# Output projection of a switch-head attention layer: turned and projected two chunks at a time, one turn per expert

## The chip, the cores and the metric

The kernel runs on one core of a Trainium2 chip. The metric is device time in microseconds (us): from a launch to its end, taken as the median of several executions. One further execution was recorded by the hardware profiler; all instruction times below come from that one and are counted from the start of its span.

## The reference, cut to what matters

Two sequences (B = 2) of T = 2048 positions with D = 256 features. The first layer is a recurrent network over blocks of 128 positions; its result is `x1`. The second layer, where the change lies, is attention with H = 8 heads of width DH = 64 whose values and outputs go through E = 5 experts:

```python
v = einsum('bthe,btek->bhtk', wv, xv)           # values: mix of the experts chosen per head
probs = softmax(q @ k.T)                        # per head, over all 2048 positions
attn = einsum('bhij,bhjd->bihd', probs, v)
out = einsum('bthe,bthk,ekd->btd', mask_o, attn, Wo)
x = x1 + out
```

The last einsum is what the change rewrites. For each position, `y[e, k]` is the sum over heads of `mask_o[h, e] * attn[h, k]`: 5 x 64 = 320 numbers. The output row is these 320 numbers times `Wo`, seen as a 320 x 256 matrix, plus `x1`.

## The kernel before, in words

**Tiles and stages.** A chunk is 128 positions; a sequence has NCH = 16 of them. A unit is one head and one block of 512 queries (4 chunks), so there are 64 units: 32 for each sequence, the 8 heads in order, 4 blocks in each head. The attention runs as a software pipeline of NT = 256 turns, 4 turns for each unit, written out by hand (`tc.manual_schedule()`), so the order of instructions on each engine is the order of the program. In every turn:

- TensorE makes two score tiles (`scores`, L642). Their matmuls contract 64 rows and make 32 columns: two halves of the array's rows and four groups of its columns, eight tiles of the array in all.
- ScalarE copies the scores out of PSUM (`stage`, L654) and VectorE keeps a running maximum (`largest`, L664).
- GpSimd or VectorE subtracts the maximum (`subtract`, L710) and ScalarE takes the exponential (`exponential`, L713), both for tiles made LAG = 6 turns earlier.
- TensorE multiplies by the values (`products`, L723; tiles of 128 rows by 32 columns, four of them), and every second turn adds up the softmax's denominator (`sums`, L744, same tile shape, into the one PSUM buffer "d").
- GpSimd issues a DMA that adds one exponentiated tile onto its neighbour (`fold`, L735), so `sums` needs half as many matmuls; `sums` waits for that DMA.

**End of a unit.** `take` and `take_sums` move the products and the denominator from PSUM to SBUF tile `os`. `close` (through `weigh`) transposes `os`, divides, and multiplies by the output masks (`masked`, L789), giving `pro`, 128 positions x 4 chunks x 5 experts x 64. For the first seven heads `gather` adds `pro` to a DRAM buffer `yd` by DMA; for the eighth, `fetch_y` loads the sum so far into `y`, and `gather` adds `pro` to it on GpSimd (L846).

**The output of a chunk.** `turn_out` transposes `y` of one chunk, 320 columns, in pieces of 128, 128 and 64 (three TensorE transposes, L859, into PSUM tile `py`), and ScalarE copies the pieces to `yT` (L863 for the two full ones, L866 for the half one). `yT` is one of two fixed buffers in SBUF pool "big". `turn_out` also issues the load of `z`, the chunk of `x1`, on SyncE's queue, unless it was loaded ahead (`load_z`, tile `zz`, four chunks at once). `project_out` then runs 3 x 4 matmuls of 128 rows by 32 columns on `wo` (L885) into `pz`, VectorE adds `z` (L893), and SyncE's queue stores the result (L894).

**Where this stands in the order.** Four tables (`before`, `between`, `first_behind`, `behind`) hold extra calls for a turn. Calls in `before` come ahead of the turn's products, calls in `behind` after them. The outputs of the first sequence are made between turns 126 and 142. Those of the second begin in turns 254 and 255 and end in `drain()`, a hand-written list after the last turn, which also finishes the last three units (called w, v and u there). The PSUM pool "m" (`misc`) has two buffers shared by all small tiles. In `drain()` the scores' PSUM is free, and a pool of four more buffers (`other`, tag "z") takes its place; the flag `spare` tells the two cases apart. `close_last` finishes the last unit and interleaves it with the last chunks' outputs.

**Queues.** SyncE's queue is in order: loads and stores wait in it for what they need, and everything behind waits too. GpSimd's fold DMAs stand in line with its subtractions in the same way.

Of the kernel before, what the change touches and what calls it, by code (L numbers as in the profile page):

```python
# [14 lines left out]
P = 128  # L15
# [5 lines left out]
def pass_over(  # L21
# [50 lines left out]
    yd = dram.tile([B, T // 512, P, 4, E, DH], F32, name="yd" + mark)  # L72
# [27 lines left out]
    wo = const.tile([P, (ED + P - 1) // P, D], F32, name="wo")  # L100
# [6 lines left out]
    wo_rows = Wo.rearrange("e k d -> (e k) d")  # L107
    o_chunks = [(i, min(P, ED - i)) for i in range(0, ED, P)]
    nc.vector.memset(wo[:, len(o_chunks) - 1, :], 0.0)
    for i, (r0, n) in enumerate(o_chunks):  # L110
        nc.sync.dma_start(out=wo[0:n, i, :], in_=wo_rows[r0 : r0 + n, :])
# [454 lines left out]
    big = ctx.enter_context(tile_pool(name="big", bufs=1))  # L566
# [23 lines left out]
    def experts(b, c):  # L590

        pv = misc([P, E, DH], f"pv{b}_{c}")
        by_quarters(pv.rearrange("p e k -> p (e k)"), b, c, wv.rearrange("p c e k -> p c (e k)"))
        xw = ap.tile([P, DH, E], F32, tag="xw", bufs=2, name=f"xw{b}_{c}")
        nc.scalar.copy(xw, pv.rearrange("p e k -> p k e"))
        nc.sync.dma_start(out=xvd[b, c // 4, :, c % 4], in_=xw)
# [191 lines left out]
    def masked(dst, po, mr, s, n):  # L788
        nc.vector.tensor_tensor(  # L789
            dst,  # L790
            po[:, s : s + n, 0:DH].unsqueeze(2).to_broadcast([P, n, E, DH]),
            mr[:, s : s + n].unsqueeze(3).to_broadcast([P, n, E, DH]),
            ALU.mult,
        )

    def close(u):

        i, n = units[u]
        b, h = heads[i]
        po, mr = weigh(u)  # L800
        pr = four.tile([P, QS, E, DH], F32, tag="pro", bufs=1, name=f"pro{u}")
        masked(pr, po, mr, 0, QS)
        o_of["p", u] = pr

    def fetch_y(u):

        i, n = units[u]
        b, _ = heads[i]
        y_of[b, n] = four.tile([P, QS, E, DH], F32, tag="y", bufs=2, name=f"y{b}_{n}")
        nc.sync.dma_start(out=y_of[b, n], in_=yd[b, n])  # L810

    def close_last(u, outs):

        i, n = units[u]
        b, _ = heads[i]
        po, mr = weigh(u)
        y = y_of[b, n]
        pr = four.tile([P, QS, E, DH], F32, tag="pro", bufs=1, name=f"pro{u}")
# [29 lines left out]
    yT_of = {"n": 0}  # L848
# [5 lines left out]
    def turn_out(b, c):  # L854
        yf = y_of[b, c // QS][:, c % QS].rearrange("p e k -> p (e k)")
        py = other(f"py{b}_{c}")[:, : len(o_chunks) * P] if spare else misc([P, len(o_chunks) * P], f"py{b}_{c}")
        py = py.rearrange("p (k n) -> p k n", n=P)
        for k, (r0, m) in enumerate(o_chunks):
            nc.tensor.transpose(py[0:m, k, :], yf[:, r0 : r0 + m], ident)  # L859
        yT = yT_all[yT_of["n"] % 2]  # L860
        yT_of["n"] += 1
        full = sum(m == P for _, m in o_chunks)
        nc.scalar.copy(yT[:, 0:full, :], py[:, 0:full, :])  # L863
        for k, (r0, m) in enumerate(o_chunks):
            if m < P:
                nc.scalar.copy(yT[0:m, k, :], py[0:m, k, :])  # L866
        z = yT_of.pop(("z", b, c), None)
        if z is None:
            z = ap.tile([P, D], F32, tag="z", bufs=3, name=f"z{b}_{c}")
            nc.sync.dma_start(out=z, in_=x1d[c, :, b, :])  # L870
        yT_of[b, c] = (yT, z)
# [8 lines left out]
    def project_out(b, c, at_end=False):  # L880
        yT, z = yT_of.pop((b, c))
        pz = other(f"pz{b}_{c}")[:, :D] if at_end else misc([P, D], f"pz{b}_{c}")
        for k, (r0, m) in enumerate(o_chunks):
            for g in range(0, P, 32):
                nc.tensor.matmul(  # L885
                    pz[g : g + 32],
                    lhsT=yT[:, k, g : g + 32],
                    rhs=wo[:, k, :],
                    start=k == 0,
                    stop=k == len(o_chunks) - 1,  # L890
                    tile_position=(0, g),
                )
        nc.vector.tensor_tensor(z, pz, z, ALU.add)  # L893
        nc.sync.dma_start(out=out[b].rearrange("(n s) d -> s n d", s=NCH)[c], in_=z)  # L894
# [4 lines left out]
    def load_late(b, c):  # L899
        late["x", c] = ap.tile([P, D], F32, tag="xl", name=f"xl{b}_{c}_{len(late)}")  # L900
        nc.sync.dma_start(out=late["x", c], in_=x1d[c, :, b, :])
# [91 lines left out]
    for b in range(1, B):  # L993

        T0 = (b - 1) * H * H_T + 2 * LAG + 3
        for c in range(NCH):
            T = T0 + c // 2 * U_T
            at(behind, T - 2 + c % 2, load_late, b, c)
            at(between, T + c % 2, stats_late, b, c)
        T0 += NCH // 2 * U_T  # L1000
        for part in range(2):
            at(behind, T0 + 3, scales_late, b, part)
            T0 += U_T
        for c in range(NCH):
# [12 lines left out]
        assert T0 <= b * H * H_T  # L1017
    for u, (i, n) in enumerate(units):
# [4 lines left out]
        outs = [(b, n * QS + s) for s in range(QS)]  # L1023
# [6 lines left out]
        if h == H - 1 and n < NQ - 3:  # L1030
            T = T1 + LAG + 4
            for o, t, p in zip(outs, (0, 1, 3, 3), (1, 2, 3, 4)):
                if T + t < NT:
                    at(before if o[1] % QS == 2 else behind, T + t, turn_out, *o)
                if T + p < NT:
                    at(behind if o[1] % QS == 2 else before, T + p, project_out, *o)
        if h == H - 1 and b < B - 1 and n >= NQ - 3:
            T = T1 + LAG + 4
            for o, t, p in zip(outs, (0, 1, 3, 3), (1, 2, 3, 4)):
                at(before if o[1] % QS == 2 else behind, T + t, turn_out, *o)  # L1040
                at(behind if o[1] % QS == 2 else before, T + p, project_out, *o)

    def drain():
# [4 lines left out]
        outs = [(B - 1, c) for c in range(NCH)]  # L1048
        turned, projected = 2, 1

        def turn(n=1):
            nonlocal turned
            for _ in range(n):
                turn_out(*outs[turned])
                turned += 1

        def project(n=1):
            nonlocal projected
            for _ in range(n):
                project_out(*outs[projected])  # L1060
                projected += 1

        load_z(B - 1, NQ - 3)
        load_z(B - 1, NQ - 2)
        spread_max(v)
        turn_max(u)
# [16 lines left out]
        turn()  # L1083
# [8 lines left out]
        turn()  # L1092
        fetch_y(v)
        project()
        load_z(B - 1, NQ - 1)
# [13 lines left out]
        turn()  # L1109
# [9 lines left out]
        project()  # L1119
# [20 lines left out]
        turn()  # L1140
        project()
        turn()
        close_last(u, outs[-QS - 2 :])
# [117 lines left out]
```

## Time and profile before

| | us |
|---|---|
| median of 3 runs | 1560.38 (1559.92 to 1560.54) |
| profiled execution, its own time | 1562.38 |
| its span | 1560.5 |
| TensorE busy | 1513.2 |
| VectorE busy | 1300.0 |
| GpSimd busy | 1287.0 |
| ScalarE busy | 1245.4 |
| 384 matmuls of the output projection, mean of one record | 0.379 |

A matmul in float32 is recorded as two instructions, so the 384 matmuls of L885 stand as 768. Matmuls overlap: what one costs is not its recorded duration but the distance between the starts of the groups. "Idle before, releaser" in a row names what ended the wait of an engine. The granted TensorE clock (PEclk) is given as a share of full speed.

### The profile page before, as it was taken

The page shows a single profiled execution, that of the slowest core. Times are in us where ns is not written, and L with a number is a line of the kernel's source. Part 1 is how long each engine was busy: PE and PEld are TensorE (multiplying, and loading weights), DVE is VectorE, ACT ScalarE, POOL GpSimd, SP SyncE. Part 2 cuts the span into 40 slices and gives each one's busy share as a digit, 9 for nine tenths or more (in the row PEclk, how much of TensorE's full clock was granted, in tenths as well). Part 3 has the DMA queues.
Part 4 walks back from the last instruction along what each step waited for, and adds up shares of the span by engine and source line. Part 5 has one row for each costly group of instructions (what it writes and reads, how often), then busy time and mean ns, then how long its engine had stood idle before and what let it go on. Part 6 is the DMA issues. An engine that isn't in the chain of part 4 may idle for free.

```text
span 1560.5 us, 41474 instructions
## 1 busy us (share of the span) xinstructions
PE 1513.2 (97%) x17582; PEld 534.4 (34%) x17582; DVE 1300.0 (83%) x1811; ACT 1245.4 (80%) x1617; POOL 1287.0 (82%) x855
## 2 busy tenths in 40 slices
PE   6999899999999999999999999999999999999988
PEld 5984222222233333333223332222222222222233
DVE  7474899999988877888987779999999999899873
ACT  4674688888888888888887778888888888888863
POOL 3154699999999987999997778899999999999970
PEclk9999999999999999999999999999999999999999
DMA  5021478888888887788786777888888888888963
GB/s 167 1 109 40 114 163 196 190 189 176 177 178 179 183 183 162 163 178 179 160 200 156 167 161 176 175 178 176 175 177 179 175 179 180 174 170 176 195 163 92
DMA packets 86821, 254.15 MB, mean 163 GB/s; under 512 B 11808, under 2 KB 31072, under 8 KB 86624
## 3 DMA queue, kind: packets, MB, share of 16 engines
q0 software_dynamic: 43488, 164.65, 57.9%
q1 hardware_dynamic: 41504, 86.13, 16.6%
q8 instruction: 140, 2.29, 0.6%
q10 hardware_dynamic: 1632, 0.61, 0.2%
q14 instruction: 57, 0.47, 0.1%
HBM read 59.46 MB, written 50.33 MB: 70 GB/s over the span
## 4 chain that ended last, share of the span: by engine, by line
PE 63%; DVE 19%; ACT 7%; issue 5%; DMA 3%; POOL 1%; ACTq 0%; SPq 0%; DVEq 0%; POOLq 0%
PE s L642 21%; PE o L723 17%; DVE m L664 11%; ACT p L654 5%; PE d L744 4%; DVE pro L789 3%; PE pq L166 3%; PE pk L147 3%; PE pz L885 2%; PE phb L368 2%; PE px L309 1%; PE pha L368 1%; DMA p<-p 1%; DMA z<-x1d 1%; ACT p L713 1%
## 5 line engine op out<-in xcount | busy, mean ns | idle before, releaser
L710 POOL TENSOR_TENSOR p<-p,top 128x1024 f32<-128x1024 f32 x378 | 1005.1, 2759 | 25.8 <-ACT top L703 25.5
L654 ACT COPY p<-s 128x1024 f32<-128x1024 f32 x512 | 511.5, 1012 | 139.6 <-issue 60.8
L713 ACT ACTIVATE p<-p 128x1024 f32<-128x1024 f32 x512 | 538.8, 1064 | 51.3 <-DVE p L710 42.7
L642 PE MATMUL s<-q,k 64*32 64x512 f32 x4096 | 501.6, 596 | 4.9 <-ACT p L654 2.5
L642 PE MATMUL s<-qs,k 64*32 64x512 f32 x4096 | 501.6, 596 | 3.5 <-ACT p L654 1.8
L723 PE MATMUL o<-p,v 128*32 128x512 f32 x4096 | 492.4, 598 | 5.1 <-DVE os L760 4.3
L664 DVE TENSOR_TENSOR m<-s,m 128x1024 f32<-128x1024 f32 x320 | 390.7, 1221 | 85.5 <-PE s L642 76.1
L735 POOL DMA_DIRECT2D p<-p x254 | 259.9, 1023 | 103.2 <-issue 43.7
L723 PEld LDWEIGHTS o<-p,v 128*32 128x32 f32 x4096 | 114.0, 109 | 301.5 <-issue 158.9
L642 PEld LDWEIGHTS s<-q,k 64*32 64x32 f32 x4096 | 100.5, 106 | 156.0 <-ACT p L654 60.3
L642 PEld LDWEIGHTS s<-qs,k 64*32 64x32 f32 x4096 | 100.4, 106 | 154.2 <-ACT p L654 58.1
L710 DVE TENSOR_TENSOR p<-p,pt 128x1024 f32<-128x1024 f32 x126 | 152.4, 1210 | 0.0
L744 PE MATMUL d<-p,ones 128*32 128x512 f32 x1032 | 136.3, 592 | 1.6 <-DMA p<-p 1.6
L664 DVE TENSOR_TENSOR m<-s,p 128x1024 f32<-128x1024 f32 x64 | 78.4, 1225 | 50.5 <-ACT p L654 49.6
L789 DVE TENSOR_TENSOR pro<-po,mr 128x1280 f32<-128x1280 f32 (+1 forms) x67 | 95.9, 1431 | 3.2 <-DVE mr L785 0.5
L626 DVE TENSOR_TENSOR xq<-xq,wp 128x1280 f32<-128x1280 f32 x60 | 89.2, 1487 | 2.1
L632 DVE TENSOR_REDUCE v<-xq 128x256 f32<-128x1280 f32 x60 | 88.5, 1475 | 0.0
L166 PE MATMUL pq<-xn2T,wq 128*32 128x512 f32 x512 | 62.2, 598 | 0.0
L147 PE MATMUL pk<-xn2T,wk 128*32 128x512 f32 x512 | 61.5, 598 | 0.0
L744 PEld LDWEIGHTS d<-p,ones 128*32 128x32 f32 x1032 | 34.0, 110 | 79.9 <-issue 76.0
L843 POOL DMA_DIRECT2D yd<-pro x48 | 60.1, 1252 | 0.0
L403 POOL TENSOR_TENSOR x<-x,hvb 128x512 f32<-128x512 f32 x14 | 17.8, 1275 | 45.8 <-ACT hs L376 34.2
(178 smaller groups left out, 1492.3 us busy)
## 6 DMA issues: line engine op xcount, KB each, us to landing
p<-p POOLq DMA_DIRECT2D x254, 512.0 KB, 5.4
xq<-xvd SPq DMA_DIRECT2D x60, 640.0 KB, 4.3
yd<-pro POOLq DMA_DIRECT2D x48, 640.0 KB, 6.5
qs<-q SPq DMA_DIRECT2D x64, 128.0 KB, 4.8
yd<-pro SPq DMA_DIRECT2D x8, 640.0 KB, 5.9
y<-yd SPq DMA_DIRECT2D x8, 640.0 KB, 8.2
x<-in_x SPq DMA_DIRECT2D x16, 256.0 KB, 5.8
x1d<-x SPq DMA_DIRECT2D x16, 256.0 KB, 2.0
```

The lines of the kernel that those rows point to most:

```text
L147: nc.tensor.matmul(pk[at_col : at_col + 32], lhsT=wk[:, kc, h * DH + g : h * DH + g + 32], rhs=xc[:, kc, c0 // 2 : (c0 + HC) // 2, o, :], ...
L166: nc.tensor.matmul(pq[at_col : at_col + 32, :], lhsT=wq[:, kc, h * DH + g : h * DH + g + 32], rhs=xn2T[:, kc, b, n * QB : (n + 1) * QB], s ...
L626: nc.vector.tensor_tensor(xq, xq, wp.unsqueeze(2).to_broadcast([P, 4, DH, E]), ALU.mult)
L642: nc.tensor.matmul(ss[g : g + 32, o, :], lhsT=k_of[i][half, c, g : g + 32], rhs=q_of[i, n][o][half, :], start=True, stop=True, tile_positi ...
L654: nc.scalar.copy(p, ss)
L664: nc.vector.tensor_tensor(m, ss, ring[t - 1] if c == 1 else m, ALU.max)
L710: eng.tensor_tensor(p, p, top.unsqueeze(1).to_broadcast([P, 2, QB]), ALU.subtract)
L713: nc.scalar.activation(ring[t], ring[t], AF.Exp)
L723: nc.tensor.matmul(o_of[u][at_col : at_col + 32, :], lhsT=v_of[i][:, 2 * c + o, g : g + 32], rhs=ring[t][:, o, :], start=c == 0, stop=c == ...
L735: nc.gpsimd.dma_start(out=ring[t], in_=ring.pop(t + 1), accum_op=ALU.add)
L744: nc.tensor.matmul(den_of[u][32 * g : 32 * (g + 1), :], lhsT=ones32, rhs=ring[(t, t1)[g // 2]][:, g % 2, :], start=first, stop=last, tile_ ...
L789: nc.vector.tensor_tensor(dst, po[:, s : s + n, 0:DH].unsqueeze(2).to_broadcast([P, n, E, DH]), mr[:, s : s + n].unsqueeze(3).to_broadcast ...
```

## The change

Outputs are made for pairs of chunks. Four things change together.

- **Layout.** `pro`, `y` and `yd` are ordered expert, chunk, 64 instead of chunk, expert, 64. So for one expert two neighbouring chunks lie side by side: 128 columns.
- **One turn per expert.** `turn_out` does one transpose of 128 columns per expert, five for a pair: the first chunk's 64 land on partitions 0 to 63, the second chunk's on 64 to 127. They are made in two parts (experts 0 to 2, experts 3 and 4), with one ScalarE copy each.
- **Projection on row halves.** `wo` holds every expert's 64 rows twice, on partitions 0 to 63 and on 64 to 127. `project_out` makes both chunks at once: for each expert, one chunk's four matmuls on the upper half of the array's rows and the other's on the lower half, into two PSUM buffers: 40 matmuls of 64 rows by 32 columns for a pair instead of 24 of 128 by 32.
- **Buffers and order.** `yT` takes space of other tags ("sg" in the turns, ring "p0" in the drain), `xw`, `z` and the late input tiles share one tag "w" of four buffers, the pool "big" is gone. The extra calls stand in a table `PLACES`; in the turns one of the two projections puts its second chunk in the denominators' buffer "d". In `drain()` the calls are reordered: `x1` of chunks 2 and 3 is loaded at its start (`load_z1`), the other loads of `x1` come later, and the addition `y + pro` of unit v runs on VectorE instead of GpSimd. `close_last` makes its two pairs ready two chunks at a time.

```diff
-    yd = dram.tile([B, T // 512, P, 4, E, DH], F32, name="yd" + mark)
+    yd = dram.tile([B, T // 512, P, E, 4, DH], F32, name="yd" + mark)
...
-    wo = const.tile([P, (ED + P - 1) // P, D], F32, name="wo")
+    wo = const.tile([P, E, D], F32, name="wo")
...
-    nc.vector.memset(wo[:, len(o_chunks) - 1, :], 0.0)
-    for i, (r0, n) in enumerate(o_chunks):
-        nc.sync.dma_start(out=wo[0:n, i, :], in_=wo_rows[r0 : r0 + n, :])
+    for p0 in range(0, P, DH):
+        nc.sync.dma_start(out=wo[p0 : p0 + DH], in_=Wo.rearrange("e k d -> k e d"))
...
-        xw = ap.tile([P, DH, E], F32, tag="xw", bufs=2, name=f"xw{b}_{c}")
+        xw = ap.tile([P, DH, E], F32, tag="w", bufs=4, name=f"xw{b}_{c}")
...
     def masked(dst, po, mr, s, n):
         nc.vector.tensor_tensor(
             dst,
-            po[:, s : s + n, 0:DH].unsqueeze(2).to_broadcast([P, n, E, DH]),
-            mr[:, s : s + n].unsqueeze(3).to_broadcast([P, n, E, DH]),
+            po[:, s : s + n, 0:DH].unsqueeze(1).to_broadcast([P, E, n, DH]),
+            mr[:, s : s + n].rearrange("p s e -> p e s").unsqueeze(3).to_broadcast([P, E, n, DH]),
             ALU.mult,
         )
...
         def ready(s):
-            masked(pr[:, s : s + 1], po, mr, s, 1)
-            nc.vector.tensor_tensor(y[:, s], y[:, s], pr[:, s], ALU.add)
+            masked(pr[:, :, s : s + 2], po, mr, s, 2)
+            nc.vector.tensor_tensor(y[:, :, s : s + 2], y[:, :, s : s + 2], pr[:, :, s : s + 2], ALU.add)
         ready(0)
-        project_out(*outs[0])
-        ready(1)
+        project_out(*outs[0], True)
+        turn_out(*outs[1])
+        ready(2)
         project_out(*outs[1], True)
-        for s in range(QS):
-            turn_out(*outs[2 + s])
-            if s + 2 < QS:
-                ready(s + 2)
-            if s:
-                project_out(*outs[1 + s], s % 2 == 0)
-        project_out(*outs[-1], True)
+        turn_out(*outs[2])
+        project_out(*outs[2], True)
...
-            nc.gpsimd.tensor_tensor(y, y, pr, ALU.add)
-    yT_all = [big.tile([P, len(o_chunks), P], F32, name=f"yT{k}") for k in range(2)]
-    for yT in yT_all:
-        nc.gpsimd.memset(yT[:, len(o_chunks) - 1, :], 0.0)
...
+            eng = nc.vector if spare and n == NQ - 2 else nc.gpsimd
+            eng.tensor_tensor(y, y, pr, ALU.add)
+    PARTS = ((0, E // 2 + 1), (E // 2 + 1, E))
+    def turn_out(b, c, parts=(0, 1)):
+        y = y_of[b, c // QS]
+        if 0 in parts:
+            if spare:
+                yT = ap.tile([P, 2, QB], F32, tag="p0", bufs=RING[0], name=f"yT{b}_{c}")
+                yT = yT.rearrange("p o q -> p (o q)")[:, : E * P].rearrange("p (e n) -> p e n", n=P)
+            else:
+                yT = ap.tile([P, E, P], F32, tag="sg", bufs=2, name=f"yT{b}_{c}")
+            yT_of[b, c] = yT
+            for o in range(2):
+                if ("z", b, c + o) not in yT_of:
+                    load_z1(b, c + o)
+        yT = yT_of[b, c]
+        for e0, e1 in [PARTS[part] for part in parts]:
+            nm = f"py{b}_{c}_{e0}"
+            py = (other(nm) if spare else misc([P, QB], nm))[:, : (e1 - e0) * P]
+            py = py.rearrange("p (e n) -> p e n", n=P)
+            for e in range(e0, e1):
+                nc.tensor.transpose(
+                    py[:, e - e0, :],
+                    y[:, e, c % QS : c % QS + 2, :].rearrange("p s k -> p (s k)"),
+                    ident,
+                )
+            nc.scalar.copy(yT[:, e0:e1, :], py)
+    def load_z1(b, c):
+        yT_of["z", b, c] = ap.tile([P, D], F32, tag="w", bufs=4, name=f"z{b}_{c}")
+        nc.sync.dma_start(out=yT_of["z", b, c], in_=x1d[c, :, b, :])
...
+    def project_out(b, c, at_end=False, sums_bank=False):
+        yT = yT_of.pop((b, c))
+        pzs = []
...
+        for e in range(E):
+            for o, pz in enumerate(pzs):
+                half = slice(o * DH, (o + 1) * DH)
+                for g in range(0, P, 32):
+                    nc.tensor.matmul(
+                        pz[g : g + 32],
+                        lhsT=yT[half, e, g : g + 32],
+                        rhs=wo[half, e, :],
+                        start=e == 0,
+                        stop=e == E - 1,
+                        tile_position=(o * DH, g),
+                    )
+        for o, pz in enumerate(pzs):
+            z = yT_of.pop(("z", b, c + o))
+            nc.vector.tensor_tensor(z, pz, z, ALU.add)
+            nc.sync.dma_start(out=out[b].rearrange("(n s) d -> s n d", s=NCH)[c + o], in_=z)
...
+    PLACES = [
+        (behind, 0, turn_out, 0, (0,)),
+        (before, 1, turn_out, 0, (1,)),
+        (before, 2, project_out, 0, False, True),
+        (behind, 3, turn_out, 2, (0,)),
+        (before, 4, turn_out, 2, (1,)),
+        (behind, 5, project_out, 2),
+    ]
...
     def drain():
...
+        for c in range(2, QS):
+            load_z1(B - 1, c)
         load_z(B - 1, NQ - 3)
-        load_z(B - 1, NQ - 2)
         spread_max(v)
+        turn()
         turn_max(u)
...
         gather(w)
-        turn()
         exponential(tu)
...
         fold(tv + 6)
-        turn()
         fetch_y(v)
-        project()
-        load_z(B - 1, NQ - 1)
+        load_z(B - 1, NQ - 2)
         take(v)
...
         exponential(tu + 4)
-        turn()
         project()
...
         turn()
-        project()
         exponential(tu + 6)
         products(tu + 4)
         products(tu + 5)
         exponential(tu + 7)
-        turn()
         fetch_y(u)
-        project()
+        load_z(B - 1, NQ - 1)
         close(v)
         gather(v)
+        project()
         products(tu + 6)
         products(tu + 7)
         take(u)
-        project()
...
         turn()
         turn()
         project()
-        turn()
-        project()
-        turn()
-        close_last(u, outs[-QS - 2 :])
+        close_last(u, outs[-3:])
```

More of the change, by code (lines that the diff above doesn't have):

```diff
@@ L106, in pass_over @@
         )
-    wo_rows = Wo.rearrange("e k d -> (e k) d")
-    o_chunks = [(i, min(P, ED - i)) for i in range(0, ED, P)]
-    nc.vector.memset(wo[:, len(o_chunks) - 1, :], 0.0)
-    for i, (r0, n) in enumerate(o_chunks):
-        nc.sync.dma_start(out=wo[0:n, i, :], in_=wo_rows[r0 : r0 + n, :])
+    for p0 in range(0, P, DH):
+        nc.sync.dma_start(out=wo[p0 : p0 + DH], in_=Wo.rearrange("e k d -> k e d"))
     ones32 = const.tile([P, 32], F32, name="ones32")
@@ L565, in pass_over @@
     RING = (LAG + 4, LAG + 3)
-    big = ctx.enter_context(tile_pool(name="big", bufs=1))
     ap = ctx.enter_context(tile_pool(name="attn", bufs=2))
@@ L800, in close @@
         po, mr = weigh(u)
-        pr = four.tile([P, QS, E, DH], F32, tag="pro", bufs=1, name=f"pro{u}")
+        pr = four.tile([P, E, QS, DH], F32, tag="pro", bufs=1, name=f"pro{u}")
         masked(pr, po, mr, 0, QS)
@@ L808, in fetch_y @@
         b, _ = heads[i]
-        y_of[b, n] = four.tile([P, QS, E, DH], F32, tag="y", bufs=2, name=f"y{b}_{n}")
+        y_of[b, n] = four.tile([P, E, QS, DH], F32, tag="y", bufs=2, name=f"y{b}_{n}")
         nc.sync.dma_start(out=y_of[b, n], in_=yd[b, n])
@@ L817, in close_last @@
         y = y_of[b, n]
-        pr = four.tile([P, QS, E, DH], F32, tag="pro", bufs=1, name=f"pro{u}")
+        pr = four.tile([P, E, QS, DH], F32, tag="pro", bufs=1, name=f"pro{u}")
         def ready(s):
-            masked(pr[:, s : s + 1], po, mr, s, 1)
-            nc.vector.tensor_tensor(y[:, s], y[:, s], pr[:, s], ALU.add)
+            masked(pr[:, :, s : s + 2], po, mr, s, 2)
+            nc.vector.tensor_tensor(y[:, :, s : s + 2], y[:, :, s : s + 2], pr[:, :, s : s + 2], ALU.add)
         ready(0)
-        project_out(*outs[0])
-        ready(1)
+        project_out(*outs[0], True)
+        turn_out(*outs[1])
+        ready(2)
         project_out(*outs[1], True)
-        for s in range(QS):
-            turn_out(*outs[2 + s])
-            if s + 2 < QS:
-                ready(s + 2)
-            if s:
-                project_out(*outs[1 + s], s % 2 == 0)
-        project_out(*outs[-1], True)
+        turn_out(*outs[2])
+        project_out(*outs[2], True)
     def gather(u):
@@ L845, in gather @@
             y = y_of[b, n]
-            nc.gpsimd.tensor_tensor(y, y, pr, ALU.add)
-    yT_of = {"n": 0}
-    yT_all = [big.tile([P, len(o_chunks), P], F32, name=f"yT{k}") for k in range(2)]
-    for yT in yT_all:
-        nc.gpsimd.memset(yT[:, len(o_chunks) - 1, :], 0.0)
[L854 to L871, printed above, removed]
+            eng = nc.vector if spare and n == NQ - 2 else nc.gpsimd
@@ new lines, in gather @@
+            eng.tensor_tensor(y, y, pr, ALU.add)
+    yT_of = {}
+    PARTS = ((0, E // 2 + 1), (E // 2 + 1, E))
[23 more added lines that the diff above has]
+            nc.scalar.copy(yT[:, e0:e1, :], py)
@@ L878, in load_z @@
             yT_of["z", b, n * QS + s] = z[:, s, :]
[L880 to L894, printed above, removed]
+    def project_out(b, c, at_end=False, sums_bank=False):
+        yT = yT_of.pop((b, c))
+        pzs = []
+        for o in range(2):
+            nm = f"pz{b}_{c + o}"
+            if at_end or o and spare:
+                pz = other(nm)[:, :D]
+            elif o and sums_bank:
+                pz = ps_o.tile([P, QB], F32, tag="d", name=nm)[:, :D]
+            else:
+                pz = misc([P, D], nm)
+            pzs.append(pz)
+        for e in range(E):
[14 more added lines that the diff above has]
+            nc.sync.dma_start(out=out[b].rearrange("(n s) d -> s n d", s=NCH)[c + o], in_=z)
     late = {}
     def load_late(b, c):
-        late["x", c] = ap.tile([P, D], F32, tag="xl", name=f"xl{b}_{c}_{len(late)}")
+        late["x", c] = ap.tile([P, D], F32, tag="w", bufs=4, name=f"xl{b}_{c}_{len(late)}")
         nc.sync.dma_start(out=late["x", c], in_=x1d[c, :, b, :])
@@ L1022, in pass_over @@
             at(first_behind, T1, spread_max, u)
-        outs = [(b, n * QS + s) for s in range(QS)]
         if T1 + LAG < NT and h == H - 1:
@@ L1029, in pass_over @@
             at(behind, T1 + LAG + 3 + (h < H - 1), gather, u)
-        if h == H - 1 and n < NQ - 3:
+        if h == H - 1 and (n < NQ - 3 or b < B - 1):
             T = T1 + LAG + 4
-            for o, t, p in zip(outs, (0, 1, 3, 3), (1, 2, 3, 4)):
+            for tab, t, f, o, *more in PLACES:
                 if T + t < NT:
[L1034 to L1041, printed above, removed]
+                    at(tab, T + t, f, b, n * QS + o, *more)
     def drain():
@@ L1047, in drain, with turn, project @@
         tv, tu = HC * v, HC * u
-        outs = [(B - 1, c) for c in range(NCH)]
-        turned, projected = 2, 1
-        def turn(n=1):
+        outs = [(B - 1, c) for c in range(0, NCH, 2)]
+        turned, projected = 1, 0
+        def turn():
             nonlocal turned
[L1053 to L1057, printed above, removed]
+            turn_out(*outs[turned])
+            turned += 1
+        def project():
             nonlocal projected
-            for _ in range(n):
-                project_out(*outs[projected])
-                projected += 1
+            project_out(*outs[projected])
+            projected += 1
+        for c in range(2, QS):
+            load_z1(B - 1, c)
         load_z(B - 1, NQ - 3)
-        load_z(B - 1, NQ - 2)
         spread_max(v)
+        turn()
         turn_max(u)
```

## The prediction

> **What bounds the kernel now.** I read the page's busy times first, then windows of the stages in which outputs are made, then TensorE's own timeline there, then the chain that ended last. The page:
>
> ```profile
> PE 1513.2 (97%) x17582; PEld 534.4 (34%) x17582; DVE 1300.0 (83%) x1811; ACT 1245.4 (80%) x1617; POOL 1287.0 (82%) x855
> PE 63%; DVE 19%; ACT 7%; issue 5%; DMA 3%; POOL 1%; ACTq 0%; SPq 0%; DVEq 0%; POOLq 0%
> ```
>
> TensorE leads, but an average says little. Four turns in which the first sequence's outputs are made (one unit, four chunks) stand here beside four ordinary turns; then come pieces of the drain. Columns: stretch, its length, busy time of each engine, granted clock, DMA share.
>
> ```profile
> core 0: us, PE busy (x) PEld busy (x) DVE busy (x) ACT busy (x) POOL busy (x), PEclk, DMA share, GB/s
> 851.90:879.70 27.80, 27.13 (x348) 10.18 (x347) 19.97 (x26) 19.64 (x28) 20.65 (x12) 1.00 0.70 162
> 973.50:993.80 20.30, 20.23 (x240) 5.82 (x236) 18.37 (x22) 17.64 (x21) 17.56 (x11) 1.00 0.69 145
> ...
> 1512.50:1518.40 5.90, 2.78 (x34) 1.49 (x36) 1.62 (x3) 1.42 (x2) 3.50 (x3) 1.00 0.90 238
> 1518.50:1521.80 3.30, 3.30 (x19) 1.02 (x12) 3.22 (x4) 1.06 (x1) 0.86 (x1) 0.50 0.95 272
> ```
>
> Outputs make the unit 7.50 us longer (27.80 - 20.30). TensorE is busy in all but 0.7 us of it; no other engine reaches 21 of the 27.80. So in these turns TensorE's instructions are the time, and what is saved there is saved at the end. The drain is different: from 1512.5 to 1518.4 TensorE works for less than half the time, and then runs at half clock. The chain of waits says why:
>
> ```profile
> 1505.66 0.35 SPq L894
> 1506.02 0.04 issue
> 1506.06 10.57 DMA z<-x1d
> ...
> 1516.72 0.25 DVE z L893
> 1516.97 0.20 issue
> 1517.18 0.70 DVE os L760
> 1517.88 0.14 issue
> 1518.02 3.27 PE o L723 x16
> ```
>
> A load of x1 sat behind a store in SyncE's queue, was issued at 1506.06 and landed 10.57 us later among folds. VectorE waited for it, `take`'s addition (L760) stood behind on VectorE, and the products of the last unit need the PSUM that it frees.
>
> **TensorE's prices**, from its timeline in turn 255:
>
> ```profile
> 1495.68 0.63 PE L642 MATMUL s<-qs,k 64*32 64x512 f32 x4
> 1496.13 0.61 PE L642 MATMUL s<-qs,k 64*32 64x512 f32 x4
> ...
> 1497.02 0.61 PE L642 MATMUL s<-q,k 64*32 64x512 f32 x4
> 1497.56 1.50 PE L885 MATMUL pz<-wo,yT 128*32 128x256 f32 x24
> 1498.88 1.90 PE L723 MATMUL o<-p,v 128*32 128x512 f32 x16
> ```
>
> Eight records of 64 rows x 32 columns x 512 start every 0.43 us, in two fours 0.03 apart. A chunk's projection takes 1.32 us until the next starts: 24 records in six groups of four, so 0.22 per group of 256 columns, half of 0.43 as the columns say. Four transposes took 0.49 (857.49 to 857.98, pt to po), 0.12 each. Where the array's tiling changes the distance is 0.54 instead of 0.43 (last scores at 1497.02 to pz at 1497.56): 0.1 per change.
>
> **In the turns, first sequence, per unit.** Before: projections 1.32 + 1.41 + 1.29 + 1.32 = 5.34; four turns of three transposes 0.44 + 0.48 + 0.45 + 0.47 = 1.84; waits ahead of transposes 0.50 + 0.17. Together 7.85, of which 7.50 is seen, so 0.35 falls into gaps that ordinary turns have anyway. After: two projections of 80 records. No row here shows 64-row tiles with 256 columns. Bounds: eight at a time as in scores, ten groups x 0.215 = 2.15 a pair; or row halves one after the other, twenty groups, 4.3. I take 2.15: the scores are the nearest row, with the same tile shape and two PSUM banks. Weight loads set no floor there: the logits' matmuls with 80 columns (L581) start a new group of four every 0.07 us. Transposes: 10 x 0.12 + 0.1 for each of four visits = 1.6. Tiling changes: [...] The old projection had the tiling of products and sums, the new one has that of scores. The row prices it at 0.1[...]. The projection ahead of products adds one change for each unit; the one behind stands next to the scores and adds none. So 4.3 + 1.6 + 0.1 = 6.0; with the waits between 0 and 0.67 (I take 0.3) and 0.35 absorbed, 6.0 to 6.6. Against 7.50 that is 0.9 to 1.5; I take 1.2. Four units: **4.8 us**.
>
> **What else moves in the turns.** `masked` writes 1280 elements in 1.49 us; only strides differ, so the same is expected; 1 ns per element more would be 1.3 us a unit, under VectorE's 1.9 us of slack (20.30 - 18.37). ScalarE: a pair's four copies (0.37 and 0.26, twice) become two (0.37, and 0.48 by interpolation to the 0.58 of 512 columns); it isn't the bound. The adds on VectorE, stores and z loads stay as many; z loads go out two at a time and two turns (over 10 us) ahead, against landings of 2.4 to 10.6 us, so the adds' waits for z (6.7 us in three) should vanish; VectorE's slack hid all but the drain's. Using the buffer "d" in the turn after take_sums and before the next sums costs a wait only if the two adds (0.42 each) slip a whole turn: nothing. Twice as many bytes for `wo` (640 KB) load at the start behind wq, wk, wv, some 700 us before use. The memsets removed were 0.2 to 0.4 us on idle engines. Shared tag "w" and changed addresses can move a first-use wait around turn 0: within 1 us either way, counted at nothing.
>
> **The drain.** TensorE from turn 255's projection to its last matmul: 1497.56 to 1554.26, 56.7 us. Work in it: 16 projections x 1.31 = 21.0; 15 turns x 0.47 = 7.0; seven pairs of products x 1.72 = 12.0; 48 records of sums = 5.2; 24 other transposes in six sets = 3.4. Sum 48.6; 8.1 are waits and slow clock. After: 8 pairs x 2.25 (a change of tiling in it) = 18.0; 37 transposes x 0.12 + 15 visits x 0.1 = 5.9; the rest as before, 20.6. Sum 44.5: **4.1 less**.
>
> The z wait: chunks 2 and 3 are now loaded at the drain's start, about 1497, free of the store in SyncE's queue, and used some ten us later. TensorE's 2.03 us of wait ahead of 1518.02 goes. Late next on VectorE is only the subtraction chain, 1.21 us a tile. With the wait goes the half clock: 16 records took 3.27 instead of 1.92, and six transposes 1.17 instead of 0.88: 1.6. So **3.6**.
>
> What stays: the sums of v wait for a fold that landed at 1513.59 (some 1.7 us before; recorded as 1.08). In the new order less TensorE work stands ahead of it, so the wait grows if it lands as late. It shares the DMA with fewer x1 loads (512 KB moved behind) but with y, 640 KB, whose fetch no longer waits for four chunks and goes out about 4 us sooner (1510.35 before). I take no change.
>
> New at the end: pairs are coarser. Turn 6 waits for `ready(0)`, which does two chunks in about 1.7 us behind two adds: 0.5 of idle TensorE. Turns 6 and 7 are each followed at once by their own projection, with a ScalarE copy (0.37 to 0.48) exposed: 0.7. And two adds follow the last matmul instead of one: 0.42. Before, 0.2 of such waits. So **1.4 more**. Addition y + pro of v on VectorE: about 1.5 us, from 0.49 for 320 elements, against 2.92 on GpSimd (L846); it stands ahead of the third pair's adds, with VectorE busy 6.2 of 16.6 us there: nothing.
>
> Drain: 4.1 + 3.6 - 1.4 = **6.3 us**. Sum with the turns 11.1: the span goes from 1560.5 to 1549.4, and as the median lies at the span within 0.1 us (the profiled execution's own 1562.38 is 1.9 above both), the median to **1549.3**.
>
> **The rivals.**
> - *The drain's wait is replaced (2 in 10).* TensorE reaches the sums of v about 1509.5 and, if the fold still lands at 1513.59, idles 4 us. The row shows the clock at half for 3.4 us after such idleness[...] 1.6 is lost again beside 2.4 more of wait: drain 2.3, total 7.1, 1553.3. By the row a 1.7 us wait kept full clock, which is my case.
> - *The fold lands early (1 in 20).* Then its 1.7 us go too, and small gaps close: 1545.
> - *The bound isn't TensorE's stream (8 in 100).* If adds, copies and PSUM "m" pace the output turns, the saved matmuls become gaps: turns 1, drain 2: 1557.4. Against: 27.13 busy of 27.80.
> - *Slower (5 in 100).* Row halves don't run together at 256 columns: 2.15 x 16 = 34 us more, 1583. It decides from a group interval of 0.285 us on (11.1 / 16 / 10 above 0.215). For: no row shows this shape; against: scores.
>
> **How the numbers follow.** The likeliest case (62 in 100) spans 1545.5 to 1552. Adding the replaced wait, partly combined with smaller turn savings, the range is 1544 to 1555.5. A difference under 0.2%, 3.1 us, can't be told from none. Faster: 0.62 + 0.20 + 0.05 + some of the third rival = 0.89; same 0.05; slower 0.06.
>
> **What would show it.** Right: L885 records in eights 0.22 us apart; output turns of one unit near 26.6 us; no VectorE wait for z in the drain; granted clock 1.00 from 1512 on; TensorE's last matmul some 7 us earlier. Wrong: fours 0.22 apart; a wait for DMA p over 3 us near 1510 with a clock of 0.50 after it; output turns still at 27.8 with "DVE z" or "ACT yT" ending TensorE's waits.

## The result, and the profile after

The changed kernel takes 1552.34 us (median of 6, 1551.69 to 1553.87); the kernel before took 1560.73 (median of 6, 1559.92 to 1561.83). The ratio is 0.9942, 95% interval 0.9932 to 0.9952: 8.4 us faster, where 11.1 were forecast; the median lies inside the stated range of 1544 to 1555.5. The page after, the two lines shown of before:

```profile
PE 1506.5 (97%) x18078; PEld 533.0 (34%) x18078; DVE 1301.1 (84%) x1807; ACT 1242.5 (80%) x1585; POOL 1284.3 (83%) x852
PE 65%; DVE 18%; ACT 7%; issue 5%; DMA 2%; POOL 1%; ACTq 0%; SPq 0%; DVEq 0%; POOLq 0%
```

TensorE has 496 more records and is busy 6.7 us less. Its share of the chain that ended last grew from 63% to 65%, the DMA's fell from 3% to 2%. By stretch: the same four turns (132 to 135) of the first sequence's outputs, then two pieces of the drain, at the same distance from turn 255's first score as the two pieces shown of before (16.8 and 22.8 us). The line ahead of the numbers names the columns.

```profile
core 0: us, PE busy (x) PEld busy (x) DVE busy (x) ACT busy (x) POOL busy (x), PEclk, DMA share, GB/s
849.90:876.64 26.74, 26.74 (x419) 10.07 (x411) 20.10 (x25) 19.26 (x25) 20.61 (x12) 1.00 0.75 176
1509.90:1515.80 5.90, 5.55 (x141) 2.92 (x133) 4.84 (x6) 3.77 (x6) 4.44 (x4) 1.00 0.91 211
1515.90:1519.20 3.30, 3.30 (x50) 0.89 (x28) 0.76 (x2) 0.03 (x1) 0.88 (x1) 1.00 1.04 227
```

The unit takes 26.74 us instead of 27.80, with TensorE busy all of it. In the drain TensorE works 5.55 of 5.90 us where it worked 2.78, and the granted clock is 1.00 where it was 0.50. TensorE's timeline in one of those turns:

```profile
851.59 0.61 PE L638 MATMUL s<-q,k 64*32 64x512 f32 x4
852.13 0.66 PE L679 MATMUL pm<-ident,mm 128*128 128x128 f32 x4
852.71 2.39 PE L899 MATMUL pz<-wo,yT 64*32 64x256 f32 x80
855.03 0.64 PE L719 MATMUL o<-p,v 128*32 128x512 f32 x4
```

A pair's projection takes 2.32 us until the next starts. Its records start in eights, 0.216 us apart; after the last eight, at 854.68, the products come 0.35 later, 0.14 more than from one eight to the next. I count that as the price of the change of tiling; no run shows it apart.

Where the time went, from the first scores of a turn to those of another. In the first row, before is the mean of five profiles of programs that share these turns (the kernel before twice, and three experiments below), after of six, with the lowest and highest in brackets. In the second row stand two profiles of the kernel before and two of the changed kernel:

| stretch | before | after | gain |
|---|---|---|---|
| turns 124 to 148, outputs of the first sequence | 152.9 (152.0 to 154.1) | 149.25 (148.5 to 149.8) | 3.6 |
| turn 255 to the end of the span | 64.8 and 61.2 | 57.5 and 57.7 | 3.6 to 7.3 |

The rest agrees: turns 148 to 255 take 542.4 to 542.6 us before and 542.2 to 542.6 after, turn 124 starts between 800.3 and 802.8 us, whatever the kernel. The two numbers for the drain before differ by 3.6 us though the program is the same; the experiments begin with them.

### The profile page after: what moved, and what is told of

Same layout as the page of the kernel before. It is cut to its first block, busy times and chain, and to the rows that moved or that the text cites. A ratio compares the mean times of both kernels' runs of the same rounds, so it can differ in the third digit from the quotient of the medians.

```text
span 1550.6 us, 42383 instructions
## 1 busy us (share of the span) xinstructions
PE 1506.5 (97%) x18078; PEld 533.0 (34%) x18078; DVE 1301.1 (84%) x1807; ACT 1242.5 (80%) x1585; POOL 1284.3 (83%) x852
## 4 chain that ended last, share of the span: by engine, by line
PE 65%; DVE 18%; ACT 7%; issue 5%; DMA 2%; POOL 1%; ACTq 0%; SPq 0%; DVEq 0%; POOLq 0%
PE s L638 22%; PE o L719 18%; DVE m L660 10%; ACT p L650 5%; PE d L740 5%; PE pk L144 3%; PE pq L163 3%; DVE pro L785 3%; PE pz L899 2%; PE phb L365 2%; PE px L306 1%; PE pha L365 1%; DMA p<-p 1%; ACT p L709 1%; PE pv L577 1%
## 5 line engine op out<-in xcount | busy, mean ns | idle before, releaser
L731 POOL DMA_DIRECT2D p<-p x254 | 264.6, 1043 | 94.4 <-issue 40.7
L400 POOL TENSOR_TENSOR x<-x,hvb 128x512 f32<-128x512 f32 x14 | 17.9, 1275 | 45.8 <-ACT hs L373 34.2
```

The costliest lines, as they stand in the source:

```text
L731: nc.gpsimd.dma_start(out=ring[t], in_=ring.pop(t + 1), accum_op=ALU.add)
```

## The experiments

**The kernel before, profiled again.** No edit.

> The kernel before, unchanged, profiled once more. Its first profiled execution took 1562.38 us, about 1.6 above its median. Theory A (the drain's stall is the same in every execution): VectorE waits again some 4.6 us for the load of x1 and the granted clock is 0.50 for about 3.3 us; span 1560 to 1561. Theory B (the stall differs between executions, and the first profile had a bad one): a shorter wait or full clock this time, span 1558 to 1559.5.

Measured: 1558.42 us, span 1556.6. The turns agree with the first profile; the drain is 3.6 us shorter. VectorE's wait for z, in its timeline, is 2.89 us instead of 4.61, and the clock stays at 1.00 from 1512 to 1518, in the row by windows:

```profile
1514.71 0.43 DVE L893 TENSOR_TENSOR z<-pz,z 128x256 f32<-128x256 f32 x1 [2.89 <-DMA z<-x1d]
1512.00:1518.00 6.00, 4.61 (x47) 1.94 (x46) 3.23 (x4) 2.50 (x5) 4.09 (x4) 1.00 0.94 252
```

So Theory B, with a span still 1.4 us shorter than it asked: the stall is there in both profiles, its size is not the same. In 25 timed executions the kernel before took 1557.85 to 1563.76 us. The execution that the prediction was made from, 1562.38, would be slower than 17 of them.

**Only the early loads of x1.**

```diff
+        for c in (2, 3):
+            z = ap.tile([P, D], F32, tag="xl", name=f"z{B - 1}_{c}")
+            nc.sync.dma_start(out=z, in_=x1d[c, :, B - 1, :])
+            yT_of["z", B - 1, c] = z
         load_z(B - 1, NQ - 3)
         load_z(B - 1, NQ - 2)
```

> The kernel before with one thing of the change: x1 of chunks 2 and 3 of the second sequence is loaded at the start of the drain (into two idle buffers). My theory (the late load of x1 stalls VectorE, then TensorE, and halves its clock): no wait for z in the drain, clock 1.00 throughout, 3.6 us faster than before, 0.9977. Rival (the stall is mostly peculiar to the profiled execution): 1.5 to 2 us, about 0.999. Rival (the fold that sums wait for takes its place): nothing.

Measured: 1560.68 us, ratio 0.9997 (0.9990 to 1.0004): nothing. The waits of its drain (who waited for whom: us in total, times, longest):

```profile
PEld d L744 <- DMA p<-p: 2.9, 1, 2.9
PE d L744 <- DMA p<-p: 2.0, 1, 2.0
```

In the kernel before the same view had these:

```profile
DVE z L893 <- DMA z<-x1d: 4.6, 1, 4.6
PEld d L744 <- DMA p<-p: 2.0, 1, 2.0
PE d L744 <- DMA p<-p: 1.1, 1, 1.1
```

The wait for z has gone from the drain, and the wait of the sums for the fold, which stood just ahead of it, has grown. The chain of waits now runs through that fold:

```profile
1504.39 10.53 DMA p<-p
1514.92 0.04 issue
1514.96 0.71 PE d L744
```

The second rival is right. The reading that this suggests, which the next run tests: two transfers were late for one reason, DMA engines busy with 512 KB pieces, and taking one of them out of the way leaves the other. The windows show the clock as well:

```profile
1512.90:1515.00 2.10, 0.09 (x4) 0.04 (x4) 1.56 (x2) 1.43 (x2) 2.10 (x2) 1.00 1.06 238
1515.20:1518.40 3.20, 3.20 (x28) 1.76 (x27) 1.28 (x2) 1.06 (x1) 1.21 (x2) 0.50 1.01 338
```

TensorE was idle for 2.01 us, and in the 3.20 us of the second row the granted clock was 0.50.

**Only the late large loads.** The kernel before, with the other half of the new load order.

```diff
         load_z(B - 1, NQ - 3)
-        load_z(B - 1, NQ - 2)
...
         fetch_y(v)
         project()
-        load_z(B - 1, NQ - 1)
+        load_z(B - 1, NQ - 2)
...
         fetch_y(u)
+        load_z(B - 1, NQ - 1)
         project()
```

> The kernel before with the other half of the drain's new load order: the second and third large loads of x1 (512 KB each) are moved behind the fetches of y for the last two units; the loads of chunks 2 and 3 stay late. With early loads of chunks 2 and 3 alone, the fold that the sums of v wait for landed 18.8 us after turn 255's start and took the stall over. Theory C (that fold's landing is the floor, and the large load ahead of it is what holds it up): it lands about 3 us sooner, the wait for z gets shorter as well since that load follows the fold; 2 to 4 us faster than before, 0.998. Theory D (the order of loads is worth nothing in this drain, the gain of the change comes from fewer matmuls alone): within 0.5 us of before.

Measured: 1557.63 us, ratio 0.9981 (0.9972 to 0.9989), 3.0 us faster. Theory C. The fold lands 14.9 us after turn 255's start instead of 17.5 to 17.9, and 6.6 us after its issue instead of 9.2 to 9.6 in the two profiles of the kernel before. TensorE's timeline where it had stood still:

```profile
1511.08 1.50 PE L885 MATMUL pz<-wo,yT 128*32 128x256 f32 x24
1512.40 1.04 PE L744 MATMUL d<-p,ones 128*32 128x512 f32 x8
1513.26 1.50 PE L885 MATMUL pz<-wo,yT 128*32 128x256 f32 x24
1514.71 1.92 PE L723 MATMUL o<-p,v 128*32 128x512 f32 x16
```

No matmul waits here. The loads of chunks 2 and 3 were left where they were and now arrive in time: they land 4.9 and 7.1 us after their issue, where they took 8.8 to 10.6 in the two profiles of the kernel before.

**Both halves of the load order.** The two edits together.

> The kernel before with both: x1 of chunks 2 and 3 at the drain's start and the two large loads behind the fetches of y. Theory C: neither z nor the fold stalls it, clock 1.00, the end of the sums falls from 39.5 to 42.8 us after turn 255's start to about 38.5; 3 to 4 us faster than before (0.9977), more than the early loads alone (0.9997). Theory D: like the early loads alone.

Measured: 1558.08 us, ratio 0.9979 (0.9971 to 0.9987); one of its 15 executions lasted 3870 us, which nothing here explains; the ratio leaves it out. No better than the late loads alone, so no gain of the early loads shows even with the large one away. The sums end 38.4 us after turn 255's start, 37.9 with the late loads alone, and 36.6 in the changed kernel.

**The order of loads, undone in the changed kernel.**

```diff
         load_z(B - 1, NQ - 3)
+        load_z(B - 1, NQ - 2)
         spread_max(v)
...
         fetch_y(v)
-        load_z(B - 1, NQ - 2)
```

> The changed kernel with the second of its three large loads of x1 (512 KB) put back to the start of the drain, ahead of two folds, where it stood before. If the DMA's order in the drain matters, the fold that the sums of v wait for lands some 2 to 3 us later than its 1507.68, TensorE waits for it, and the kernel is 2 to 3 us slower than the changed one (0.9942 of before becomes about 0.996). If not, the same as the changed kernel within 0.5 us.

Measured: 1553.52 us, ratio 0.9950 (0.9937 to 0.9964), 1.2 us above the changed kernel, with overlapping intervals. Its profile says more. The timeline of TensorE:

```profile
1506.35 1.03 PE L740 MATMUL d<-p,ones 128*32 128x512 f32 x4
1509.27 1.05 PE L740 MATMUL d<-p,ones 128*32 128x512 f32 x4 [1.90 <-DMA p<-p]
```

The fold lands 1.9 us later (16.5 instead of 14.6 after turn 255's start), TensorE waits for it, and the sums end 38.1 instead of 36.6 us after that start. So the wait comes back at a little under its forecast; with the clock at 1.00 this time, after 1.90 us of idleness. The time alone would not decide: 1.2 us lies between the two outcomes that were named.

**Row halves one after the other.** The same 40 matmuls for a pair, ordered chunk by chunk.

```diff
-        for e in range(E):
-            for o, pz in enumerate(pzs):
+        for o, pz in enumerate(pzs):
+            for e in range(E):
```

> The changed kernel with the loops of the projection swapped: all five experts of the first chunk of a pair, then all five of the second, so that only one half of the array's rows works at a time; 40 matmuls as before. Theory (two row halves at once are what makes the projection cheap): twenty groups of four, 0.216 us apart, instead of ten of eight: 2.16 us more in each of 16 pairs, 34 us slower than the changed kernel, about 1587, slower than the kernel before by 1.7%. Rival (matmuls of the second half run ahead into the idle half, or other engines set the pace): under 10 us slower than the changed kernel.

Measured: 1569.19 us, ratio 1.0052 (1.0037 to 1.0067): slower than before, as the theory says, but 17 us above the changed kernel, half of what it asks. The timeline of one projection:

```profile
853.48 0.66 PE L679 MATMUL pm<-ident,mm 128*128 128x128 f32 x4
854.07 3.71 PE L899 MATMUL pz<-wo,yT 64*32 64x256 f32 x80
857.71 1.06 PE L719 MATMUL o<-p,v 128*32 128x512 f32 x8
```

It takes 3.64 us until the next starts instead of 2.32. In one projection, followed record by record, its 80 records start in 16 groups 0.216 apart instead of 20: six of four, then four of eight, then six of four. In the four of eight the first chunk's last matmuls and the second chunk's first ones run together. So the free half of the array took up its work while up to four groups of the other half, which stand earlier in the program, were still to start; by what rule, the records don't tell. For the projections that stand behind, the first scores that follow start beside them: at 850.82, with 12 of the 80 records of the projection ahead of it still to start (8 at 851.01, 4 at 851.44). Turns 124 to 148 cost about 7 us more for their eight pairs (156.65 against 149.25), not 17. Theory and rival are each right in part: running eight at a time is what makes the pair cheap (2.32 us instead of 3.64), and it decides between faster and slower than before, but 3.64 is less than the 4.3 of twenty groups: some of the overlap is there without the order of the program.

**Without the denominators' buffer.**

```diff
-        (before, 2, project_out, 0, False, True),
+        (before, 2, project_out, 0),
```

> The changed kernel with the first pair's projection in the turns taking both of its buffers from the pool of two instead of one from the denominators' buffer. Theory: the second chunk's matmuls then wait until the maximum's transpose ahead of them is reduced by VectorE (0.69 us after it), so each of the four units of the first sequence loses about 0.8 us, 3 us in all: 1555.4, 0.996 of before. Rival (VectorE's slack hides it): same as the changed kernel.

Measured: 1556.75 us, ratio 0.9970 (0.9959 to 0.9981), about 4 us above the changed kernel by the ratios. The waits of turns 128 to 143 have two entries that the changed kernel's lack:

```profile
PEld pz L899 <- DVE mq L684: 2.8, 4, 0.7
PE pz L899 <- DVE mq L684: 0.9, 4, 0.2
```

The four units are 0.72 to 0.83 us longer each, 3.2 together, at the place foreseen. That is nearly all of what the pairs save in the turns: turns 124 to 148 take 152.6 us here, 152.9 before and 149.25 in the changed kernel. The cheaper projection pays there only because its second buffer comes from elsewhere.

**The addition back on GpSimd.**

```diff
-            eng = nc.vector if spare and n == NQ - 2 else nc.gpsimd
+            eng = nc.gpsimd
```

> The changed kernel with the addition y + pro of the last unit but one back on GpSimd (2.9 us there, 1.49 on VectorE). The transposes that need it start at 1529.6 in the changed kernel's profile, pro is ready at 1524.8: on GpSimd it would end at 1527.7. Theory (this part of the change is worth nothing): same within 0.5 us. Rival: two adds of the third pair come sooner on VectorE and the product's PSUM is freed sooner: up to 1 us faster.

Measured: 1552.78 us, ratio 0.9945 (0.9931 to 0.9958): the same. The sums end 36.67 us after turn 255's start, 36.58 in the changed kernel. No worth of this part of the change shows, as the prediction said.

**A reordered tail.** The changed kernel's end leaves TensorE idle ahead of the last two pairs (idle before, releaser, in brackets):

```profile
1536.37 0.74 PE L864 MATMUL py<-ident,y 128*128 128x128 f32 x5 [0.21 <-PE pz L899]
1537.51 2.39 PE L899 MATMUL pz<-wo,yT 64*32 64x256 f32 x80 [0.41 <-ACT yT L869]
1539.83 0.77 PE L864 MATMUL py<-ident,y 128*128 128x128 f32 x5
1540.95 2.39 PE L899 MATMUL pz<-wo,yT 64*32 64x256 f32 x80 [0.35 <-ACT yT L869]
```

```diff
         turn()
-        project()
-        close_last(u, outs[-3:])
+        close_last(u, outs[-4:])
...
         ready(0)
-        project_out(*outs[0], True)
-        turn_out(*outs[1])
+        project_out(*outs[0])
+        turn_out(*outs[2])
         ready(2)
         project_out(*outs[1], True)
-        turn_out(*outs[2])
+        turn_out(*outs[3])
         project_out(*outs[2], True)
+        project_out(*outs[3], True)
```

> The changed kernel with the last pairs reordered: the fifth pair's projection is moved behind the last unit's transposes and the two last turns each stand one projection ahead of their own, so that no ScalarE copy is exposed. The three exposures on record at the end of the changed kernel (0.21, 0.41 and 0.35 us of idle TensorE) should go: 0.9 us faster than the changed kernel, 0.9936 of before. If the end is set by VectorE's additions or the stores instead, no change.

Measured: 1550.80 us (1549.73 to 1551.46), ratio 0.9931 (0.9917 to 0.9944), 1.5 us below the changed kernel; the intervals of the ratios overlap, but the slowest of these five executions is below the fastest of the changed kernel's first six (1551.69). The same place:

```profile
1534.24 0.74 PE L865 MATMUL py<-ident,y 128*128 128x128 f32 x5
1534.91 2.41 PE L900 MATMUL pz<-wo,yT 64*32 64x256 f32 x80
1537.25 0.77 PE L865 MATMUL py<-ident,y 128*128 128x128 f32 x5
1537.95 4.73 PE L900 MATMUL pz<-wo,yT 64*32 64x256 f32 x160
```

From turn 255, TensorE ends 0.7 us earlier (49.54 instead of 50.25), and the span's end follows the last addition by 5.7 us instead of 6.5; the two make the 1.5.

**The tail and an earlier fold.** In addition:

```diff
+        fold(tv + 2)
         subtract(tv + 7)
...
         products(tv + 5)
-        fold(tv + 2)
```

> The reordered tail and, in addition, the first fold of the drain moved ahead of one GpSimd subtraction: it can be issued about 1.5 us sooner, and TensorE waits for it about 1 us in the changed kernel. If that wait is on the path: up to 1 us faster than the reordered tail alone, 0.9925 of before. If other traffic or later waits set the end: no more than the reordered tail.

Measured: 1550.39 us, ratio 0.9929 (0.9916 to 0.9943). The fold lands 1.3 us earlier (13.4 instead of 14.7), and the sums end at 36.7 instead of 36.6: no more than the reordered tail, so that last microsecond of waiting was not on the path. Between the two versions there is no difference that shows. Each median lies 1.5 to 2.2 us below those of the changed kernel, with overlapping intervals of the ratios.

**The changed kernel again.** No edit.

> The changed kernel, unchanged, timed and profiled on the same chip as the three others. 0.9942 of before; profile with a clock of 1.00 in the drain, like the first.

Measured: 1552.57 us, ratio 0.9945 (0.9932 to 0.9959). Clock 1.00 in the drain, sums 36.65 us after turn 255's start.

## Why the prediction was right, and where its steps were off

**The turns: 3.6 us instead of 4.8.** The mechanism holds: TensorE's stream is the time, the records run in eights 0.216 us apart, and the transposes fell from 96 to 80 (no run shows their share apart). Three terms of the sum were off.

- The unit that I took as the measure of before, 27.80 us, was the longest of three. The others have 27.60; in the one I took, TensorE waited 0.17 us for VectorE, which had waited 1.8 us for z.
- A projection ahead of the products costs 2.32 us, not 2.15 and 0.1 for a change of tiling: the change back to 128 rows is 0.14, and the start adds 0.02. The one behind, for which I counted 2.15, costs 2.68 in the first two units and 3.03 in the third, from its start to the first eight of the scores behind it. Both its buffers come from the pool of two, and VectorE is still reading one of them (`mh`, at L666), so that the first chunk's records start alone; in the third unit:

```profile
901.10 0.64 PE L899 MATMUL pz<-wo,yT 64*32 64x256 f32 x8
901.95 2.15 PE L899 MATMUL pz<-wo,yT 64*32 64x256 f32 x68 [0.21 <-DVE mm L666]
```

- The 0.35 us that gaps absorb were named and not taken off: with that "6.0 to 6.6" would have been about 5.6 to 6.3. This slip made up for the dearer projections. Measured, outputs make the first three units 6.2, 6.4 and 6.8 us longer than the 20.30 of ordinary turns.

The first two units gain 1.1 us each (27.60 to 26.50, 27.81 to 26.74), the third 0.5. The rest of the 3.6 is a balance: the first chunk's projection has moved from turn 127 into the turns behind, and the work now reaches one turn further. The price of a change of tiling, 0.1 us from the last scores to pz in the kernel before, was near: 0.14 of distance behind a projection of the changed kernel.

What the prediction did not reckon is the worth of the buffer "d" as a second bank: without it the turns gain about 0.3 us instead of 3.6.

**The drain's stall: right in its effect, wrong in its cause.** The step "the z wait: chunks 2 and 3 are now loaded at the drain's start" failed. Alone that edit is worth nothing. What pays is the step that I passed over with "I take no change": the fold shares the DMA with less, and lands some 3 us sooner (with the late loads alone 6.6 us after its issue instead of 9.2 to 9.6). In the changed kernel both large loads are out of its way and not one: the first is issued at 1495.59 and has landed at 1498.91, before the fold's issue at 1501.41. The chain of waits had pointed at z because z landed last; a fold just ahead of it landed nearly as late, and both had the same two large loads in front (issued at 1502.89 and 1503.70, landed at 1506.92 and 1509.76). The rival "the drain's wait is replaced" is what the early loads alone show, with 2.01 us of idle TensorE and a clock of 0.50 behind it; the changed kernel escapes it by the other half of the order. The 3.6 us are 3.0 when measured by the late loads alone. That this holds inside the changed kernel too is shown by its profile with the load put back (1.5 us in the drain), less surely by its time. That the forecast came near is luck: the change happened to hold the half that pays beside the half that I reckoned with.

**The drain's work: as reckoned.** Against the kernel before with late loads, which has no stall left, TensorE's last matmul ends 3.4 us sooner after turn 255 (53.66 to 50.25). My sum without the second addition at the end was 4.1 less work and 1.0 more in new waits: 3.1. The exposures were measured at 0.97, forecast at 1.2. With the second addition the last one ends 3.1 us sooner (54.15 to 51.04), where I had 2.7.

**What the sum lacked.** The span's end follows the last addition by 6.5 us instead of 5.6 with the late loads; the reordered tail has 5.7. The last two stores are issued close together, and the second issue took 1.51 us where a last store took 0.33; I had counted the second addition but nothing for its store. Over all profiles the two go together: last issues of 0.33 to 0.39 us with an end of 5.4 to 5.8 us, 0.70 with 6.0, 1.45 to 1.67 with 6.4 to 7.0. No run changes the issue alone.

And the execution that I read was a slow one of its kernel: 1562.38 us, 1.6 above the median of before. I took a gain read from it off the median, although part of that gain was its longer stall. That the median agreed with its span was chance: an execution's time lies 1.8 to 1.9 us above its span in all these runs (1562.38 and 1560.5, 1558.42 and 1556.6, 1552.41 and 1550.6). With 3.0 for the stall, 3.6 for the turns, 3.1 for the drain up to the last addition, less 0.9 for the end, the sum is 8.8, against 8.4 (7.5 to 10.6 by the interval).

## What to carry to other kernels

When the chain of waits ends at a DMA that landed late, look at what was in front of it on the DMA engines and what else landed late at that time: here moving the waiting load alone gave a ratio of 0.9997, because a fold was late behind the same two large loads, and putting large loads later gave 0.9981. Where a matmul stream sets the pace, count its PSUM buffers before you count the matmuls: the pairs saved 3.6 us in the turns with the buffer "d" and about 0.3 without. And price a new shape by the distance between its groups and to its neighbours: 0.216 us for an eight here, 0.1 to 0.14 more where the tiling changes. Measure a stall from more than one execution before subtracting it from a median: the two profiles of the kernel before differ by 3.6 us in the drain.

## What the runs showed of the hardware that I had not expected

- With the 20 groups of four ordered one chunk after the other, four of the first chunk's ten still ran beside the second chunk's: the projection took 3.64 us, where 20 groups 0.216 apart would take 4.3 and ten eights took 2.32. The two row halves overlapped there in part without being interleaved in the program.
- Two waits of nearly the same length left different clocks behind them. After 2.01 us of idle TensorE the clock was 0.50 (the early loads alone, 1515.20 to 1518.40), after 1.90 us it was 1.00 (the changed kernel with the load put back):

```profile
1509.61:1513.02 3.41, 3.41 (x88) 1.64 (x88) 3.36 (x4) 2.01 (x2) 3.41 (x3) 1.00 0.78 254
```

  In the prediction I had used a wait of 1.7 us at full clock as if it were a bound. What decides whether such a wait costs the clock, these two cases do not show.
- A store issued about 0.4 us behind another on SyncE's queue (0.37 to 0.46) took 0.38 to 1.59 us to issue in the changed kernel's profile. In the kernel before no two stores of outputs were issued less than 1.26 us apart, and each took 0.33 to 0.54.
